# A recurrent image layer and a state-space layer on one core: the second layer's order of issue from another table of priorities

## The chip, the cores and the metric

The kernel runs on one core of a Trainium2 chip. The metric is the device time of one execution in microseconds; the median of several runs counts. The engines are TensorE (PE, with its weight loads PEld), VectorE (DVE), ScalarE (ACT), GpSimd (POOL) and SyncE (SP), which here does nothing but issue DMAs. "us" is a microsecond.

## The reference

The input is 16 images of 64 x 64 pixels with 128 channels, in float32. Two layers follow one another, each with a group norm before and a residual sum after:

```python
x = x + L0(group_norm(x))      # a 2-D recurrent layer: 5 gates, swept along the diagonals
x = x + L1(group_norm(x))      # a state-space layer (Mamba) on the 4096 pixels in order,
                               # once forward and once backward, the two results summed
```

The change touches only the second layer. For each image and direction it computes, with 256 inner channels and 16 states:

```python
xz = x @ in_w.T;  xc, z = split(xz)
xc = silu(conv1d(xc, 4 taps))
dt, Bm, Cm = split(xc @ x_w.T);  dt = softplus(dt @ dt_w.T + dt_b)
for t in pixels:                                 # per channel d and state s
    h[d, s] = exp(-dt[t, d] * exp(A_log[d, s])) * h[d, s] + dt[t, d] * Bm[t, s] * xc[t, d]
    y[t, d] = sum_s h[d, s] * Cm[t, s]
out = ((y + xc * D) * silu(z)) @ out_w.T
```

## The kernel before

The first layer takes the first 1.6 ms and is not touched. The second layer works in passes. A pass is 512 pixels of one image in one direction, so an image has 16 passes: 0 to 7 forward, 8 to 15 backward (`second` in the code). A forward pass ends by storing its `y` (`spill`); the backward pass of the same pixels fetches it (`recall`), adds it (`again`), multiplies by the gate (`finish`), turns it (`back`) and projects it (`project`). So a backward pass has more matmuls than a forward one. During an image's forward passes the next image is read: `read_load`, `read_turn` (TensorE), `read_take` (ACT), `read_stats` (DVE), in eight chunks; then `normal` makes the norm's factors and `normalise` (ACT, L1068) applies them, chunk by chunk.

A pass has 2 halves of 128 channels (h) and 16 states (s), that is 32 scans on DVE (`scan`, L1305), each over 128 partitions x 512 pixels. Each scan needs a decay factor, which ACT makes as an exponential (`decay`, L1251, tile `da`). There are two kinds of states:

- States 0 to 3 (letter X in the plan): POOL makes the product that drives the scan (`drive`, L1259) in a tile `group`, of which there are two buffers. TensorE turns the scanned group (`turned`, L1337, tile `ptg`), ACT copies it (`turned_take`, L1345), and TensorE weighs it by Cm and sums it (`weigh`, L1352).
- States 4 to 15 (letter R): TensorE makes the drive of four states at a time (`drive_rows`, L1285, tile `hps`); DVE scans into `hst`; POOL multiplies two states by their Cm rows (`out_of`, L1328, tile `hc`); TensorE sums by transposes into `py` (`sums`, L1365).

Further operations of a pass: `conv` (TensorE, L1122, tile `pp`, two passes ahead), `silu` and `softplus` (ACT, in "sessions", since each needs its function table loaded), `xproj`, `dtproj`, `bturn`, `times` (POOL, L1232, tile `dtx`), `turn`, `skip`, `gate`. The carried states go from pass to pass by small DMAs (`keep`, `keep_group`); rows of Bm and Cm are spread over the partitions by DMAs (`spread`).

Nothing of this runs in the order of the source. When the kernel is built, `order_of_issue` makes a list of all operations of all 256 passes with what each needs, and `simulate` plays them through with a cost table and picks, whenever an engine is free, the ready operation with the smallest key whose buffers are free. The key of an operation of pass i (the image's first pass counts 16 times the images before it) is

```python
at = NS * i
urgency = at + URGENCY[name][second][args if who is None else ()]
```

So a pass is worth 16 units, a small number goes first, and an engine never idles while something for it is ready. `read_*` of chunk n have the `at` of pass n of the image before, and `normalise` of chunk k has that of pass 8 + k. The list that comes out is issued as it stands: it fixes the order in each engine's queue and in SP's queue of DMAs, and each queue is worked in that order. Buffers go round by operation order too (`RINGS`: 2 `group`, 3 `hst`, 3 `hc`, 9 `da`, 1 `quad`, 1 `xl`; three shared banks for `misc`). The order of states within a pass is a constant of its own, `ORDER`.

Of the kernel before, what the change touches and what calls it, by code (L numbers as in the profile page):

```python
# [44 lines left out]
def units_of(order):  # L45

    count = {}
    for x in order:
# [4 lines left out]
        else:  # L53
# [37 lines left out]
        {(0, 0): -19.08, (0, 1): 208.77, (0, 2): 213.67, (0, 3): 242.61, (1, 0): -194.98, (1, 1): -170.3,  # L91
         (1, 2): -208.38, (1, 3): -208.83},
        {(0, 0): 148.19, (0, 1): 250, (0, 2): 249.74, (0, 3): 231.08, (1, 0): -185.59, (1, 1): -186.03,
         (1, 2): -176.29, (1, 3): -177.49},
    ),
    "xproj": (
        {(): -6.34},
        {(): 83.3},
    ),
    "xproj_take": (  # L100
        {(): 46.52},
        {(): -25.9},
    ),
    "rows": (
        {(): 10.88},
        {(): -173.37},
    ),
    "bturn": (
        {(): 216.27},
        {(): -247.72},  # L110
    ),
    "bturn_take": (
        {(): -10.16},
        {(): 155.72},
    ),
    "dtproj": (
        {(0,): -166.35, (1,): -49.09},
        {(0,): -234.94, (1,): -199.34},
    ),
    "times": (  # L120
        {(0,): -141.19, (1,): -141.5},
        {(0,): -190.57, (1,): -223.42},
    ),
    "turn": (
        {(0,): 231.47, (1,): -199.74},
        {(0,): 155.15, (1,): 101.59},
    ),
    "turn_take": (
        {(0,): 35.4, (1,): 33.43},
        {(0,): 227.22, (1,): 227.05},  # L130
    ),
    "skip": (
        {(0,): -85.09, (1,): 194.24},
        {(0,): -59.43, (1,): 211.98},
    ),
    "spread": (
        {("b", 0): 55.31, ("d", 0): 221.01, ("c", 0): 249.78, ("c", 1): 249.59, ("d", 1): -104.59, ("c",
         2): 74.43, ("c", 3): 179.65, ("b", 1): 235.3, ("d", 2): 178.23, ("c", 4): 117.53, ("c", 5):
         216.75, ("k", 0): 205.82},
        {("b", 0): 49.04, ("d", 0): 82.05, ("c", 0): 58.5, ("c", 1): 225.69, ("d", 1): 85.64, ("c", 2):  # L140
         -52.53, ("c", 3): -84.56, ("b", 1): -71, ("d", 2): 188.69, ("c", 4): -46.09, ("c", 5): 139.95,
         ("k", 0): 79.7},
    ),
    "drive": (
        {(0, 0): -117.16, (1, 0): -45.65, (0, 1): -106.02, (1, 1): 204.54},
        {(0, 0): -55.01, (1, 0): -101.65, (0, 1): 78.56, (1, 1): 78.33},
    ),
    "decay": (
        {(0, 0): 214.71, (4, 0): 231.6, (5, 0): 235.97, (6, 0): 250, (7, 0): 244.04, (1, 0): -226.9, (8,
         0): 242.45, (9, 0): 229.56, (10, 0): 250, (11, 0): 196.68, (2, 0): 245.22, (12, 0): 142.99, (13,  # L150
         0): 196.62, (14, 0): 218.85, (15, 0): 250, (3, 0): 235.27, (4, 1): 237.55, (5, 1): 56.83, (6,
         1): 236.39, (7, 1): 200.04, (0, 1): 59.98, (8, 1): 241.45, (9, 1): 238.35, (10, 1): 238.37, (11,
         1): 237.94, (1, 1): 48.96, (12, 1): 223.29, (13, 1): 109.79, (14, 1): 109.58, (15, 1): 193.48,
         (2, 1): 244.06, (3, 1): 190.67},
        {(0, 0): 219.27, (4, 0): 159.93, (5, 0): 228.42, (6, 0): 227.96, (7, 0): 233.04, (1, 0): 162.12,
         (8, 0): 236.54, (9, 0): 145.98, (10, 0): -139.12, (11, 0): -88.73, (2, 0): -99.75, (12, 0):
         157.46, (13, 0): 250, (14, 0): 156.85, (15, 0): 167.22, (3, 0): 239.69, (4, 1): 187.28, (5, 1):
         236.16, (6, 1): 225.96, (7, 1): 248.99, (0, 1): 67.98, (8, 1): 248.77, (9, 1): 49.99, (10, 1):
         242.8, (11, 1): 168.72, (1, 1): 67.45, (12, 1): 163.7, (13, 1): 244.57, (14, 1): 244.31, (15,
         1): 176.22, (2, 1): 178.59, (3, 1): 181.09},  # L160
    ),
    "scan": (
        {(0, 0): -215.99, (4, 0): -197.78, (5, 0): -201.82, (6, 0): 171.7, (7, 0): -200.28, (1, 0):
         208.99, (8, 0): 81.27, (9, 0): 69.78, (10, 0): 50.84, (11, 0): 80.97, (2, 0): -179.33, (12, 0):
         -157.48, (13, 0): -159.07, (14, 0): -158.42, (15, 0): -158.71, (3, 0): -148.7, (4, 1): 17.61,
         (5, 1): 34.08, (6, 1): 7.6, (7, 1): 7.23, (0, 1): 145.62, (8, 1): 26.88, (9, 1): 56.47, (10, 1):
         26.63, (11, 1): 52.08, (1, 1): 203.51, (12, 1): 173.49, (13, 1): 174.73, (14, 1): 173.35, (15,
         1): 173.11, (2, 1): 173.02, (3, 1): -185.61},
        {(0, 0): 211.65, (4, 0): 208.82, (5, 0): 213.32, (6, 0): 210.34, (7, 0): 234.88, (1, 0): 234.81,
         (8, 0): 82.08, (9, 0): 81.92, (10, 0): 11.04, (11, 0): 61.9, (2, 0): 80.26, (12, 0): 96.06, (13,  # L170
         0): 93.07, (14, 0): 44.04, (15, 0): 82.19, (3, 0): 68.39, (4, 1): -115.05, (5, 1): -159.13, (6,
         1): -144.43, (7, 1): -169.42, (0, 1): -152.48, (8, 1): -158.76, (9, 1): -192.29, (10, 1):
         -192.53, (11, 1): -193.7, (1, 1): 178.94, (12, 1): 148.84, (13, 1): 136.94, (14, 1): 136.65,
         (15, 1): 184.35, (2, 1): 182.44, (3, 1): 227.69},
    ),
    "scatter": (
        {("d", 0): -98.3, ("d", 1): 226.02, ("d", 2): -35.02, ("k", 0): 142.02},
        {("d", 0): 197.57, ("d", 1): 181.75, ("d", 2): -137.41, ("k", 0): 53.02},
    ),
    "drive_rows": (  # L180
        {(0, 0): 86.02, (1, 0): -84.84, (2, 0): 123.21, (0, 1): 206.34, (1, 1): 117.75, (2, 1): 194.74},
        {(0, 0): 241.28, (1, 0): -59.19, (2, 0): -162.71, (0, 1): -157.55, (1, 1): -215.22, (2, 1):
         175.52},
    ),
    "keep": (
        {(0, 0): 250, (1, 0): -11.9, (2, 0): 227.54, (3, 0): -221.6, (4, 0): 195.72, (5, 0): -92.62, (0,
         1): 62.29, (1, 1): 169.33, (2, 1): 81.35, (3, 1): -229.04, (4, 1): 142.26, (5, 1): -18.73},
        {(0, 0): -186.63, (1, 0): 100.75, (2, 0): 123.12, (3, 0): -226.46, (4, 0): 126.26, (5, 0):
         182.78, (0, 1): -126.19, (1, 1): 179.51, (2, 1): -247.02, (3, 1): -146.55, (4, 1): -45.3, (5,
         1): 57.7},  # L190
    ),
    "out_of": (
        {(0, 0): 6.28, (1, 0): 110.81, (2, 0): 0.41, (3, 0): 46.99, (4, 0): 204.64, (5, 0): 230.6, (0,
         1): 26.46, (1, 1): 164.53, (2, 1): -138.94, (3, 1): -244.66, (4, 1): -239.51, (5, 1): -149.12},
        {(0, 0): -174.66, (1, 0): -174.81, (2, 0): 72.48, (3, 0): 7.85, (4, 0): 129.81, (5, 0): 102.68,
         (0, 1): -122.95, (1, 1): -122.04, (2, 1): -117.06, (3, 1): -192.11, (4, 1): -39.91, (5, 1): 57.1},
    ),
    "sums": (
        {(0, 0): 147.01, (1, 0): 204.95, (2, 0): 18.42, (3, 0): 110.12, (4, 0): -165.71, (5, 0): -154.21,
         (0, 1): 227.07, (1, 1): 180.09, (2, 1): 194.99, (3, 1): 242.48, (4, 1): 216.64, (5, 1): -169.16},  # L200
        {(0, 0): -212.32, (1, 0): -162.81, (2, 0): -161.63, (3, 0): -161.82, (4, 0): -157.85, (5, 0):
         -158.54, (0, 1): 73.85, (1, 1): 109.31, (2, 1): 81.83, (3, 1): 248.19, (4, 1): 249.43, (5, 1):
         249.81},
    ),
    "keep_group": (
        {(0, 0): -194.35, (0, 1): -163.44},
        {(0, 0): -239.33, (0, 1): -182.43},
    ),
    "turned": (
        {(0, 0, 0): -203.27, (0, 0, 1): 190.03, (0, 0, 2): 9.82, (0, 0, 3): -96.4, (0, 1, 0): 229.53, (0,  # L210
         1, 1): -154.5, (0, 1, 2): -157.58, (0, 1, 3): -113.93},
        {(0, 0, 0): -157.81, (0, 0, 1): 123.6, (0, 0, 2): -144.76, (0, 0, 3): -39.63, (0, 1, 0): 248.86,
         (0, 1, 1): 248.61, (0, 1, 2): 248.52, (0, 1, 3): 239.67},
    ),
    "turned_take": (
        {(0, 0, 0): 113.8, (0, 0, 1): 75.95, (0, 0, 2): 42.34, (0, 0, 3): 42.24, (0, 1, 0): 247.32, (0,
         1, 1): 153.61, (0, 1, 2): 153.43, (0, 1, 3): 222},
        {(0, 0, 0): 64.54, (0, 0, 1): 69.77, (0, 0, 2): 68.43, (0, 0, 3): 67.62, (0, 1, 0): -249.7, (0,
         1, 1): -214.46, (0, 1, 2): 155.94, (0, 1, 3): 155.85},
    ),  # L220
    "weigh": (
        {(0, 0): -250, (0, 1): -131.3},
        {(0, 0): -179.49, (0, 1): -150.84},
    ),
    "finish": (
        {(0,): 43.55, (1,): 250},
        {(0,): -158.64, (1,): 234.04},
    ),
    "spill": (
        {(): 111.19},  # L230
        {},
    ),
    "read_load": (
        {(): -159.46},
        {},
    ),
    "read_turn": (
        {(): 120.8},
        {},
    ),  # L240
    "read_take": (
        {(): 144.64},
        {},
    ),
    "read_stats": (
        {(): 1.05},
        {},
    ),
    "gate": (
        {},  # L250
        {(0,): -158.22, (1,): -164.04},
    ),
    "recall": (
        {},
        {(): -141.83},
    ),
    "again": (
# [1238 lines left out]
```

## Time and profile before

| | us |
|---|---|
| median of 3 runs | 12678.93 (12673.02 to 12680.4) |
| the profiled execution, its own time | 12716.73 |
| its span, first to last instruction | 12714.9 |
| first `times` of the second layer | 1580.8 after the start |
| pass 9 to 14 of any image from 1 to 14, each | 43.98 |

The TensorE clock granted is 0.993 of full speed over the span. In the second layer the profile's engine totals per 1000 us are about 960 us for PE, 905 for DVE, 835 for ACT and 932 for POOL. The profile's tables by stretch have a line for each stretch of time: its bounds and length, then busy time and number of instructions of PE, PEld, DVE, ACT and POOL, then the granted PE clock, the share of DMA engines and GB/s. A line of a timeline has the start, the time from the start of the first to the end of the last of a run of like instructions, engine, source line, tiles and count, and in brackets the idle time before it and what ended it. PE's instructions overlap: a matmul that is shown with 275 ns can start 109 ns after the one before it.

### The profile page before, as it was taken

Reading aid. Unit: us, or ns where it says so; the run is one execution under the profiler, and the core shown is the slowest. Engines: PE = TensorE matmul, PEld = TensorE weight load, DVE = VectorE, ACT = ScalarE, POOL = GpSimd, SP = SyncE. Lnnn points to the kernel's source line nnn. Section 1 sums busy time; section 2 is a strip of 40 time slices with the busy share of each in tenths; the row PEclk is TensorE's granted clock in tenths of the full one; section 3 lists DMA queues with packets and bytes.
Section 4 is the critical chain, followed back from the end, with each engine's and each line's share of the span. In section 5 each row is a group of like instructions: output and inputs, shape, how many; then the busy total and the mean of one; then the engine's idle time right before and its main releaser. Section 6 shows DMA issues by size and latency. Waiting matters only on the chain. (4 is left out here: it accounts for less than half of the span.)

```text
span 12714.9 us, 322475 instructions
## 1 busy us (share of the span) xinstructions
PE 12144.3 (96%) x128820; PEld 9452.5 (74%) x128820; DVE 11120.1 (87%) x11409; ACT 9944.8 (78%) x15935; POOL 10600.8 (83%) x4868
## 2 busy tenths in 40 slices
PE   8999999999999999999999999999999999999999
PEld 7666777777777777777777777777777777777777
DVE  6676599998989899999999998999989898989998
ACT  3444488888888888888888888888888888888887
POOL 0111199999999999999999998999999999999998
PEclk8999999999999999999999999999999999999999
DMA  4222155555555555555555555555555565556564
GB/s 151 54 57 55 49 157 162 159 159 158 164 160 156 160 161 158 159 165 156 164 159 160 158 164 158 163 161 156 160 159 160 156 163 156 158 158 164 155 163 138
DMA packets 2320784, 1885.93 MB, mean 148 GB/s; under 512 B 1537697, under 2 KB 1883313, under 8 KB 2319281
## 3 DMA queue, kind: packets, MB, share of 16 engines
q1 hardware_dynamic: 2241328, 1830.04, 52.2%
q10 hardware_dynamic: 77952, 35.24, 1.2%
q8 instruction: 1017, 16.66, 0.5%
q14 instruction: 487, 3.98, 0.1%
HBM read 1698.25 MB, written 164.30 MB: 146 GB/s over the span
## 5 line engine op out<-in xcount | busy, mean ns | idle before, releaser
L1328 POOL TENSOR_TENSOR hc<-hst,cr 128x1024 f32<-128x1024 f32 x3072 | 7380.5, 2430 | 416.6 <-DVE hst L1305 308.6
L1305 DVE TENSOR_TENSOR_SCAN hst<-da,carry,hps 128x512 f32<-128x512 f32 x5376 | 6452.1, 1261 | 497.7 <-issue 266.5
L1251 ACT ACTIVATE da<-dt,A_log_sb 128x512 f32<-128x512 f32 x8192 | 5386.9, 710 | 907.0 <-DVE hst L1305 814.8
L1365 PEld LDWEIGHTS py<-ident,hc 128*128 128x128 f32 x24576 | 2760.8, 141 | 685.1 <-issue 322.3
L1365 PE MATMUL py<-ident,hc 128*128 128x128 f32 x24576 | 3136.2, 275 | 139.2 <-POOL hc L1328 135.8
L1259 POOL TENSOR_TENSOR group<-dtx,br 128x1024 f32<-128x1024 f32 x1024 | 2448.6, 2405 | 150.2 <-PE ptg L1337 80.0
L1305 DVE TENSOR_TENSOR_SCAN group<-da,carry,group 128x512 f32<-128x512 f32 x1792 | 2236.1, 1267 | 203.7 <-ACT da L1251 199.5
L1285 PEld LDWEIGHTS hps<-d,dtxt 32*128 32x128 f32 x49152 | 1522.7, 186 | 731.7 <-issue 389.2
L1285 PE MATMUL hps<-d,dtxt 32*128 32x128 f32 x49152 | 1804.9, 283 | 211.1 <-DVE hst L1305 128.3
L1122 PE MATMUL pp<-xT,wk 128*128 128x512 f32 x4096 | 1994.7, 600 | 2.4 <-ACT dt L1226 1.2
L1345 ACT COPY ht<-ptg 128x512 f32<-128x512 f32 x2048 | 1130.4, 588 | 414.8 <-PE ptg L1337 390.3
L889 POOL TENSOR_TENSOR a_f<-a_f,c 128x288 f32<-128x288 f32 (+40 forms) x254 | 211.3, 832 | 1338.2 <-ACT a_f L881 1272.4
L1337 PE MATMUL ptg<-ident,group 128*128 128x128 f32 x8192 | 1154.3, 276 | 50.2 <-DVE group L1305 27.0
L1337 PEld LDWEIGHTS ptg<-ident,group 128*128 128x128 f32 x8192 | 926.5, 141 | 273.5 <-issue 106.2
L1122 PEld LDWEIGHTS pp<-xT,wk 128*128 128x128 f32 x4096 | 681.6, 191 | 420.6 <-issue 390.4
L1305 DVE TENSOR_TENSOR_SCAN hst<-da,hps 128x512 f32<-128x512 f32 x768 | 876.3, 1200 | 124.4 <-POOL hc L1328 38.2
L1232 POOL TENSOR_TENSOR dtx<-dt,xc 128x512 f32<-128x512 f32 x512 | 650.4, 1286 | 198.1 <-ACT dt L1226 168.2
L1251 ACT ACT_TABLE_LOAD x527 | 676.1, 1283 | 9.7
L1365 PE MATMUL py<-ddiag,xc 128*128 128x128 f32 x4096 | 579.3, 284 | 12.3 <-ACT y L1412 11.3
L1352 PE MATMUL py<-ht,k 128*32 128x128 f32 x16384 | 557.7, 276 | 0.8
L1365 PEld LDWEIGHTS py<-ddiag,xc 128*128 128x128 f32 x4096 | 496.8, 191 | 54.4 <-ACT y L1412 15.6
L1216 PE MATMUL pv<-dbl,dt_wT 128*128 128x256 f32 x2048 | 531.2, 392 | 0.2 <-DVE st L1056 0.2
(112 smaller groups left out, 12155.8 us busy)
## 6 DMA issues: line engine op xcount, KB each, us to landing
cr<-rows SPq DMA_DIRECT2D x1536, 512.0 KB
d<-d SPq DMA_DIRECT2D x768, 448.0 KB
br<-rows SPq DMA_DIRECT2D x512, 512.0 KB
k<-k SPq DMA_DIRECT2D x256, 256.0 KB
yf<-y SPq DMA_DIRECT2D x128, 512.0 KB
yl<-yf SPq DMA_DIRECT2D x128, 512.0 KB
carry<-hst SPq DMA_DIRECT2D x3072, 1.0 KB
xs<-in_x_dram SPq DMA_DIRECT2D x64, 512.0 KB
```

What stands on the lines that cost most here:

```text
L1122: nc.tensor.matmul(self.ps["conv", h], lhsT=wk[:, k, h * P : (h + 1) * P], rhs=xT[self.b % 2][:, t0 : t0 + T], start=(k == 0), stop=(k == ...
L1216: nc.tensor.matmul(pv[:, q * TQ : (q + 1) * TQ], lhsT=dt_wT[:, q, h * P : (h + 1) * P], rhs=self.dbl, start=True, stop=True,)
L1232: nc.gpsimd.tensor_mul(self.dtx[h], self.dt[h], self.xc[h])
L1251: nc.scalar.activation(t, self.dt[h], AF.Exp, scale=amat[:, h, s : s + 1])
L1259: nc.gpsimd.tensor_mul(both[:, m : m + 2, :], bc(self.dtx[h], 1, 2), self.brow[q])
L1285: nc.tensor.matmul(part[:, j, :, :], lhsT=self.dtxt[h][rows, j, :], rhs=dg[rows, j + r, :, :], start=True, stop=True, skip_group_check=True,)
L1305: nc.vector.tensor_tensor_scan(t[:, self.rev], self.da.pop((s, h))[:, self.rev], dbx[:, self.rev], 0.0 if self.first else carry[:, self.d, ...
L1328: nc.gpsimd.tensor_mul(self.hc[g, h], self.hst[g, h].rearrange("p t m -> p m t"), self.crow[g])
L1337: nc.tensor.transpose(pt[:, k, :], self.group[g, h][:, t0 : t0 + TB, :].rearrange("p t s -> p (t s)"), ident,)
L1345: nc.scalar.copy(t, self.ps.pop(("turned", g, h, j)))
L1352: nc.tensor.matmul(self.py[h][q * TB : (q + 1) * TB, j * P : (j + 1) * P], lhsT=cd[:, GX * j + q, :], rhs=self.ht[g, h, j][:, q, :], start ...
L1365: nc.tensor.matmul(self.py[h][:, cols], **{"start": False, "stop": False, **how}, skip_group_check=True)
```

## The change

The table `URGENCY` gets other numbers, nearly all of them. Names, arguments and meaning of the entries, the operations, the cost table, buffers and `ORDER` stay as they are; so do the instructions of every engine, but for their order. Of the diff, the entries that the text below speaks of (in each entry the first table is for forward passes, the second for backward ones):

```diff
     "drive": (
-        {(0, 0): -117.16, (1, 0): -45.65, (0, 1): -106.02, (1, 1): 204.54},
-        {(0, 0): -55.01, (1, 0): -101.65, (0, 1): 78.56, (1, 1): 78.33},
+        {(0, 0): -56.91, (1, 0): -57.77, (0, 1): 215.02, (1, 1): 247.85},
+        {(0, 0): 171.33, (1, 0): 123.34, (0, 1): 160.79, (1, 1): 118.53},
     ),
     "decay": (
-        {(0, 0): 214.71, (4, 0): 231.6, (5, 0): 235.97, (6, 0): 250, (7, 0): 244.04, (1, 0): -226.9, (8,
...
+        {(0, 0): 224.88, (4, 0): 226.48, (5, 0): 240.06, (6, 0): 188.37, (7, 0): 250, (1, 0): 113.5, (8,
...
     "scan": (
-        {(0, 0): -215.99, (4, 0): -197.78, (5, 0): -201.82, (6, 0): 171.7, (7, 0): -200.28, (1, 0):
-         208.99, (8, 0): 81.27, (9, 0): 69.78, (10, 0): 50.84, (11, 0): 80.97, (2, 0): -179.33, (12, 0):
-         -157.48, (13, 0): -159.07, (14, 0): -158.42, (15, 0): -158.71, (3, 0): -148.7, (4, 1): 17.61,
-         (5, 1): 34.08, (6, 1): 7.6, (7, 1): 7.23, (0, 1): 145.62, (8, 1): 26.88, (9, 1): 56.47, (10, 1):
-         26.63, (11, 1): 52.08, (1, 1): 203.51, (12, 1): 173.49, (13, 1): 174.73, (14, 1): 173.35, (15,
-         1): 173.11, (2, 1): 173.02, (3, 1): -185.61},
...
+        {(0, 0): -110.99, (4, 0): -110.09, (5, 0): -105.1, (6, 0): -105.34, (7, 0): -105.61, (1, 0):
+         181.32, (8, 0): 19.6, (9, 0): 19.21, (10, 0): -80.71, (11, 0): 7.49, (2, 0): 40.13, (12, 0):
+         -108.17, (13, 0): -102.34, (14, 0): -10.85, (15, 0): -108.25, (3, 0): -48.47, (4, 1): -48.83,
+         (5, 1): -68.91, (6, 1): -83.82, (7, 1): -96.92, (0, 1): -31.74, (8, 1): -33.58, (9, 1): -38.05,
+         (10, 1): -40.96, (11, 1): -50.07, (1, 1): 200.94, (12, 1): -50.19, (13, 1): -87.76, (14, 1):
+         -88.26, (15, 1): -91.09, (2, 1): -5.51, (3, 1): -86.39},
...
     "read_load": (
-        {(): -159.46},
+        {(): 20.22},
...
     "read_turn": (
-        {(): 120.8},
+        {(): 64.91},
...
     "read_take": (
-        {(): 144.64},
+        {(): 21.14},
...
     "read_stats": (
-        {(): 1.05},
+        {(): -142.37},
...
     "normal": (
...
-        {(): 74.69},
+        {(): 29.66},
...
     "normalise": (
...
-        {(): 57.35},
+        {(): 32.48},
...
     "session": (
-        {(0,): 241.85, (1,): 239.93},
-        {(0,): 173.19, (1,): 69.9},
+        {(0,): 219.11, (1,): 226.41},
+        {(0,): 244.88, (1,): 9.25},
```

## The prediction

> **What bounds the kernel now.** I read the page first (engine totals), then busy time by stretch, one stretch per pass of the second layer, cut where POOL starts the pass's first `dtx` product (L1232); then the timeline of all engines in the worst pass, and TensorE's timeline in a backward pass. The page says only that four engines are nearly full:
>
> ```profile
> span 12714.9 us, 322475 instructions
> PE 12144.3 (96%) x128820; PEld 9452.5 (74%) x128820; DVE 11120.1 (87%) x11409; ACT 9944.8 (78%) x15935; POOL 10600.8 (83%) x4868
> ```
>
> The stretches say which of them bounds which pass. They are passes 1, 2, 6, 7, 8 and 10 of image 8; columns: length, busy PE, PEld, DVE, ACT, POOL.
>
> ```profile
> 7163.04:7209.38 46.34, 41.61 (x484) 32.86 (x480) 40.54 (x39) 37.52 (x61) 40.77 (x20) 1.00 0.68 185
> 7209.38:7256.80 47.42, 41.16 (x475) 31.68 (x474) 41.28 (x40) 44.32 (x69) 40.43 (x19) 1.00 0.50 144
> 7380.15:7420.60 40.45, 38.55 (x456) 30.17 (x456) 37.62 (x33) 34.28 (x55) 40.45 (x20) 1.00 0.59 159
> 7420.60:7462.46 41.86, 38.38 (x456) 30.11 (x456) 38.98 (x34) 35.48 (x55) 40.49 (x19) 1.00 0.57 160
> 7462.46:7509.24 46.78, 43.29 (x518) 33.66 (x518) 40.25 (x36) 35.49 (x57) 45.27 (x21) 1.00 0.58 161
> 7553.22:7597.20 43.98, 43.97 (x496) 34.76 (x492) 40.16 (x36) 36.35 (x56) 40.64 (x18) 1.00 0.56 161
> ```
>
> See three regimes. A forward pass in its stride (the third and fourth lines) is POOL's: POOL works 40.45 to 40.49 us of it and the pass lasts 40.45 to 41.86. A backward pass (the last) is TensorE's: 43.97 us busy of 43.98, and six passes of every image have that length to 0.06 us. Passes 1, 2 and 8, where the direction turns, belong to nobody: no engine fills them. The last image has no successor to read, and its passes 1 and 2 are shorter:
>
> ```profile
> 12039.14:12082.49 43.35, 38.81 (x462) 30.42 (x458) 39.30 (x35) 36.36 (x57) 40.42 (x20) 1.00 0.58 158
> 12082.49:12122.92 40.43, 38.73 (x456) 30.23 (x456) 37.38 (x33) 33.85 (x54) 40.43 (x19) 1.00 0.60 162
> ```
>
> So reading and normalising the next image is what stretches passes 1 and 2. How it does so, in pass 2 of image 8:
>
> ```profile
> 7226.80 3.62 ACT L1068 ACTIVATE xT<-xT,shift_l,scale_l 128x512 f32<-128x512 f32 x5
> ...
> 7231.03 2.51 DVE L1305 TENSOR_TENSOR_SCAN group<-da,carry,group 128x512 f32<-128x512 f32 x2 [0.52 <-ACT da L1251]
> ...
> 7233.60 0.66 PE L1337 MATMUL ptg<-ident,group 128*128 128x128 f32 x4 [0.79 <-DVE group L1305]
> ...
> 7237.86 2.38 POOL L1259 TENSOR_TENSOR group<-dtx,br 128x1024 f32<-128x1024 f32 x1 [4.74 <-PE ptg L1337]
> ```
>
> Five normalisations in a row hold ACT; the scans of `group` wait for their decay, TensorE's turns wait for the scans, and POOL's next `drive` waits 4.74 us for one of two `group` buffers.
>
> **The change, part by part.** No instruction is added or removed; every engine's queue is put in another order, DMA issue on SP included. So the cost of an edit is not a duration but what becomes late, and I cost it by regime, per image, from the means of images 1 to 14 in the same stretches: pass 0 38.45; passes 1 and 2 94.66; passes 3 to 7 206.62; pass 8 47.80; passes 9 to 14 263.90; pass 15 44.12; in all 695.55 us.
>
> *Backward passes 9 to 15.* TensorE cannot be better fed: the gain is nothing unless its own work shrinks. It can change a little, since a switch between kinds of matmul has a price:
>
> ```profile
> 7564.11 1.02 PE L1122 MATMUL pp<-xT,wk 128*128 128x512 f32 x2
> 7565.07 1.17 PE L1285 MATMUL hps<-d,dtxt 32*128 32x128 f32 x32
> ...
> 7567.10 1.02 PE L1122 MATMUL pp<-xT,wk 128*128 128x512 f32 x2
> 7567.96 0.60 PE L1337 MATMUL ptg<-ident,group 128*128 128x128 f32 x4
> ```
>
> A pair of `pp` takes 0.96 us of the queue ahead of the 32-row `hps`, 0.86 us ahead of `ptg`, which keeps the shape: 0.10 us for a switch. A backward pass has 17 switches (counted in its list). I can't see how many the new order has; two more or fewer a pass are 0.2 x 7 x 16 = 22 us, of either sign; I take 0. The Trainium skill speaks against treating an order of matmuls as free: "TensorEngine Tiling (Array Packing)", Key Properties, says that a change of tiling mode drains the engine. The row agrees and gives the price; the page has none. On headroom the skill and the row differ: "Perfetto Trace Analysis", Identifying the Most-Contended Engine, would judge TensorE by its weight loads and not by matmul busy time. By that, 34.76 of 43.98 us, an estimate of 9.2 us a pass could still be had by a better order, 9.2 x 7 x 16 = 1030 us in all. I don't count it: the batches of this timeline follow one another at the same distance wherever they stand (0.87 to 0.96 us for eight `py` of 128 columns, the longer ones beside a switch, and once 1.04), which is how a full queue looks.
>
> *Forward passes 3 to 7.* 206.62 less five times POOL's 40.5 us is 4.1 us an image that a perfect order would give. A loss is as possible: TensorE works 38.4 to 38.9 us of these passes, so it has only some 1.9 us to give before POOL starves. I take 0.
>
> *Pass 8.* 47.80 us with POOL busy for 45.27: at most 2.5 us. I take 0.
>
> *Passes 1 and 2.* 94.66 against 83.78 in the last image: 10.9 us an image are the price of the next image's reading, of which the work itself would fit beside POOL (POOL's own 81 us are a floor 13.7 us below). The table moves this part most visibly. `normal` (DVE) goes from 74.69 to 29.66 while most forward scans move to between -111 and 40, so at pass 2 its key, 128 + 29.66 = 158, stands behind nearly all scans (32 + 40 = 72 or less), where it stood at 203 ahead of those at 32 + 209 = 241 and 32 + 204 = 236. That is for a gain: scans are no longer held up by it. Against it: `normalise` goes from 57.35 to 32.48, so for chunk k its key at pass 2 is 160 + 16k, and with decays of that pass at 32 + 225 = 257 seven chunks come ahead of decay (0, 0), where four did (185 + 16k against 247): the same burst on ACT, 7 x 0.70 = 4.9 us by the 3.62 us row. The ends are 0 and 10.9 us; neither row is nearer, since the last image leaves the whole of the work out and not only its bunching, and I take half, 5.4 us, in 15 images: 82 us.
>
> *Start and end.* The first image's passes 0 and 1 take 79 us together, near two of POOL's; the last pass and the tail take 85 us after POOL's last `dtx`. I take 0 for both; a few us are possible.
>
> The sum: the profiled execution's own time is 12716.73 us, of which the span is 12714.9. 12716.7 - 82 = 12635. The median of the runs is 12678.93, 0.997 of it, so 12635 x 0.997 = 12597 us.
>
> **The rivals.** *More than half.* If the new order spreads the burst and also straightens the forward passes, the ceiling is 13.7 + 4.1 + 2.5 = 20.3 us an image, 305 us in 15 images; 10.9 + 3.3 (half of the other two) give 213 us, or 12467 us. For it: POOL, TensorE and DVE each have the room in passes 1 and 2. Against it: one `xl` buffer and two `group` buffers stay, and the keys of `normalise` keep the burst.
>
> *Slower: TensorE's queue starves POOL in the forward passes.* The queue is in order; a `py` or `ptg` batch that waits for POOL or DVE holds back the `hps` behind it, then the scans, then POOL. The planner that made the order bills TensorE too little: its cost table adds up to 42.64 us for a backward pass, where the row shows 43.98, and to 36.7 for a forward one, where the rows show 38.4 to 38.9. It therefore sees 4.0 us of room in a forward pass (40.7 of its own POOL costs) where there are 1.9, and a longer search uses up room that it believes in. The point from which this decides is a hold-up of over 1.9 us a pass. Its price by the nearest rows, the 1.35 us that POOL waits for `hst` twice in pass 1: one such wait in each of passes 3 to 7 is 1.35 x 5 x 16 = 108 us, 12679 + 108 = 12787 us. For it: three engines are over 90% busy there. Against it: the present order, made with the same costs, stays within 1 us of POOL's floor.
>
> *Nothing.* The keys move but work goes wherever an engine is idle, so the bunching and the floors stay: 12679 us, give or take 25.
>
> *A stall in backward passes.* DVE, POOL and ACT have 3.3 us or more to spare there, so one extra wait is absorbed; 0.5 us a pass would be 56 us, 12735.
>
> **How the numbers follow.** What a measurement of this kernel can tell from no change is about 0.2%, 25 us. The forecast, a gain from 25 to some 165 us (12515 to 12654 is its own range), has 0.44; the larger gain 0.13; nothing 0.14; the slower forward passes 0.22; the backward stall 0.07. Faster is 0.57, the same 0.14, slower 0.29. The range runs from the larger gain's 12467 to just over the forward rival's 12787: 12465 to 12800, and I leave some 0.06 below and 0.1 above.
>
> **What would show it.** In the profile after: passes 1 and 2 together at about 89 us instead of 94.66, with POOL's longest wait on `ptg` under 4.74; passes 9 to 15 still 43.9 to 44.2 us with TensorE busy throughout; passes 3 to 7 still within 40.5 to 42.5. Wrong would be: backward passes under 43.5 (the work of TensorE is not fixed) or over 44.5 (it is no longer fed); forward passes over 42.5 (the slower rival); or equal busy and idle times everywhere.

## The result, and the profile after

The changed kernel takes 12606.47 us in the median of 4 runs (12602.26 to 12615.94), the kernel before 12676.69 us in the runs beside them (12673.02 to 12680.4). The ratio is 0.9945, with a 95% interval from 0.9932 to 0.9959: 70 us or 0.55% faster. The forecast was 12597 us, with all of its gain in passes 1 and 2. The size came out right, by luck: in two profiles taken for comparison (below), passes 1 and 2 give 22 of 62 us, and most of the gain lies elsewhere.

The page of the changed kernel hides the change as well as that of before did. Its span and engine totals:

```profile
span 12600.5 us, 322464 instructions
PE 12132.4 (96%) x128820; PEld 9488.3 (75%) x128820; DVE 11138.1 (88%) x11409; ACT 9942.7 (79%) x15935; POOL 10601.1 (84%) x4868
```

The busy time by stretch, for the same six passes of image 8 as in the prediction (1, 2, 6, 7, 8 and 10; columns: length, busy PE, PEld, DVE, ACT, POOL, PE clock, DMA share, GB/s):

```profile
7114.09:7159.33 45.24, 41.19 (x480) 32.33 (x477) 40.77 (x39) 38.14 (x61) 40.54 (x20) 1.00 0.66 184
7159.33:7206.28 46.95, 42.59 (x478) 33.93 (x476) 41.01 (x40) 43.58 (x69) 40.47 (x20) 0.96 0.57 151
7330.66:7371.48 40.82, 38.52 (x456) 30.13 (x456) 38.62 (x33) 35.04 (x55) 40.48 (x19) 1.00 0.60 159
7371.48:7412.53 41.05, 38.84 (x456) 30.15 (x456) 38.29 (x33) 35.19 (x55) 40.53 (x20) 1.00 0.57 162
7412.53:7457.73 45.20, 43.36 (x506) 33.83 (x506) 40.41 (x36) 35.78 (x57) 45.20 (x21) 1.00 0.57 167
7501.50:7545.19 43.69, 43.66 (x496) 34.88 (x492) 40.22 (x36) 36.34 (x57) 40.66 (x18) 1.00 0.58 161
```

Passes 1 and 2 lost about a microsecond and a half together, where 5.4 were forecast. Pass 8 went from 46.78 to 45.20 us, which is POOL's own busy time, so in this image no wait of POOL is left there. The backward pass is still TensorE's alone (43.66 of 43.69), but it is 0.29 us shorter with the same 496 matmuls. The PE clock in pass 2 is 0.96, where the lines of before have 1.00; an experiment below follows this up.

The timeline of pass 2 shows the picture of before again, a little worse at its end:

```profile
7176.19 3.62 ACT L1066 ACTIVATE xT<-xT,shift_l,scale_l 128x512 f32<-128x512 f32 x5
...
7180.42 1.28 DVE L1303 TENSOR_TENSOR_SCAN group<-da,carry,group 128x512 f32<-128x512 f32 x1 [1.75 <-ACT da L1249]
...
7187.35 2.39 POOL L1257 TENSOR_TENSOR group<-dtx,br 128x1024 f32<-128x1024 f32 x1 [5.24 <-PE ptg L1335]
```

The burst of `normalise` on ACT, the scan that waits for its decay, and POOL's wait for a `group` buffer are all there. POOL's wait is 5.24 us, where 4.74 stood before and less was forecast.

### The profile page after: what moved, and what is told of

The parts are those of the page before. It is cut to its first block, busy times and chain, and to the rows that moved or that the text cites. A ratio compares the mean times of both kernels' runs of the same rounds, so it can differ in the third digit from the quotient of the medians.

```text
span 12600.5 us, 322464 instructions
## 1 busy us (share of the span) xinstructions
PE 12132.4 (96%) x128820; PEld 9488.3 (75%) x128820; DVE 11138.1 (88%) x11409; ACT 9942.7 (79%) x15935; POOL 10601.1 (84%) x4868
## 5 line engine op out<-in xcount | busy, mean ns | idle before, releaser
L1120 PE MATMUL pp<-xT,wk 128*128 128x512 f32 x4096 | 1954.9, 599 | 1.7 <-ACT dt L1224 1.2
```

The source lines that it names most:

```text
L1120: nc.tensor.matmul(self.ps["conv", h], lhsT=wk[:, k, h * P : (h + 1) * P], rhs=xT[self.b % 2][:, t0 : t0 + T], start=(k == 0), stop=(k == ...
```

## Where the time went

The first profiled execution of before lay 40 us above its median, so I measured both kernels again and compare these two executions. In the experiments the kernel before runs at 12736 us, 0.5% above the first comparison; ratios are therefore compared, not times. The unchanged copies:

> The kernel before, unchanged, profiled a second time. Its first profiled execution took 12716.7 us, 40 us over the median of its other runs, so the profiles of before and after stand 114 us apart where the medians stand 70. If the 40 us are chance of that one execution, the second one takes 12665 to 12690 us and it is seen where they lay (forward passes 3 to 7 below 206.6 us an image, or the tail below 85 us). If the profile itself costs them, it takes 12710 to 12720 again. In both cases the backward passes 9 to 14 stay at 43.98 us.

Measured: 0.9995 of the kernel before [0.9985, 1.0005], span 12726.0 us. The profiled execution took 12727.8 us, above both values named, but not longer than the other executions of the same copy (median 12730). So the profile itself costs nothing here; what the first one's 40 us were stays open. The backward passes stayed at 43.98 us.

> After, unchanged, for a second profile and a second measure of its gain. The forward passes 3 to 7 took 204.7 us an image in its first profile; with one batch moved in backward passes alone (the second dtproj behind drive_rows), on another chip, they took 207.4, as before's did there (207.5). If the order itself shortens these passes, they are at least 1.5 us shorter than before's again wherever both are profiled; if that difference was chance of the execution, they lie anywhere from 204.5 to 207.5, while passes 9 to 13 (43.70), pass 8 (45.5 to 46.1 against 47.6 to 47.8) and the 72 us after POOL's last dtx come back. Ratio to before 0.993 to 0.996.

Measured: 0.9945 [0.9931, 0.9959] over five runs, span 12664.2 us, 61.8 us less. I cut both traces at POOL's first `dtx` of every pass and take means over images 1 to 14:

| stretch | before again, us | changed again, us | per image | all 16 images | forecast |
|---|---|---|---|---|---|
| passes 1 and 2 | 94.61 | 93.28 | -1.33 | -22 | -82 |
| of these, pass 1 | 47.09 | 46.06 | -1.03 | -17 | |
| of these, pass 2 | 47.51 | 47.23 | -0.28 | -5 | |
| passes 3 to 7 | 207.45 | 207.05 | -0.40 | -9 | 0 |
| pass 8 | 47.57 | 46.25 | -1.32 | -24 | 0 |
| passes 9 to 15 | 308.04 | 307.78 | -0.26 | -4 | 0 |
| up to the second layer's first `dtx` | 1581.9 | 1579.5 | | -2 | 0 |

The column for all images adds the first and the last image, which I measured by themselves. The rows for passes 3 to 7 can't be trusted to the microsecond: five executions of before's order gave 206.6 to 207.5 us there and six of the changed order 204.7 to 207.6. Passes 1 and 2 are firm: 94.61 to 94.81 against 93.18 to 93.28 us. So is pass 8 in its sign: 47.5 to 47.8 against 45.5 to 46.5 us. (Copies that an experiment below edits in another place are counted with their order.)

The gain of passes 1 and 2 lies in pass 1. In the first two profiles too, pass 1 went from 47.22 to 45.62 us and pass 2 from 47.44 to 47.61. What shrank in pass 1 is a wait of TensorE, which reads the next image's chunks there through the one `xl` buffer and stands until each chunk has landed: 2.30 us an image in before's second profile, 1.50 in the changed kernel's (2.46 and 1.17 in the first two). The sixth chunk of image 8, before and after:

```profile
7193.97 0.63 PE L1046 MATMUL pt<-ident,xl 128*128 128x128 f32 x4 [0.88 <-DMA xl<-x]
```

```profile
7144.26 0.60 PE L1044 MATMUL pt<-ident,xl 128*128 128x128 f32 x4
```

In each of the 14 profiles of this study pass 1 is longer in those images where this wait is longer, by 0.8 to 1.5 us for each microsecond. No experiment changes this wait alone, so that it is the cause fits the traces and isn't shown.

## The experiments

An execution's whole list of operations is made before anything is issued. Most edits below only move entries of that list, by a small generator `rearranged` around `order_of_issue(B)`; the diffs, shortened, show what it moves. Three questions were open: what holds passes 1 and 2, why a backward pass is shorter, and what happened in pass 8.

**Is it the burst of `normalise`?** The changed kernel, with the eight steps moved to passes 3 to 10, one each:

```diff
+        if name == "normalise":
+            held[who, args[0]] = op
+            continue
+        if name == "turned_take" and args == (0, 1, 0):
+            b, i = divmod(who, NP)
+            if (b + 1, i - 2) in held:
+                yield held.pop((b + 1, i - 2))
```

> After, with the eight normalisations of the next image moved in ACT's queue from one burst in pass 2 to one chunk in each of passes 3 to 10, in front of the ACT copies of turned state group (0, 1). Theory A, that of the prediction (the burst holds back the decays, then the group scans, the turns and POOL, which waits 5.2 us on ptg in pass 2): pass 2 falls from 47.6 us to about 44 and the wait on ptg to under 2 us, the other passes stay; 15 images x 3.6 = 54 us, so about 12550 us. Theory B (not the burst but the norm's short chain before it and the reading itself stretch passes 1 and 2): pass 2 changes by less than 1 us, passes 3 to 10 lose up to 0.7 us each, so 12600 to 12690 us.

Measured: 0.9933 [0.9916, 0.9949]; passes 1 and 2 together 91.67 us instead of 93.28 (pass 2 45.94 instead of 47.23), passes 3 to 7 206.86, pass 8 46.06. In pass 2 VectorE's wait for the decay fell from 2.58 to 0.53 us, as the chain in the prediction has it, but POOL's wait on `ptg` only from 5.14 to 4.21. The burst is worth 1.3 us an image in pass 2, 1.6 with pass 1, not half of 11. By its median this is the fastest kernel of the study; its interval overlaps that of the changed kernel, so that it beats it isn't shown.

**Is it the root with its table loads, or the statistics?** In the first of the two kernels the norm's square is made by VectorE and the square root is left out from image 1 on; in the second, seven of the eight statistics of an image are left out.

```diff
-        nc.scalar.activation(std, pv, AF.Sqrt, bias=eps)
-        nc.vector.reciprocal(scale, std)
+        nc.vector.reciprocal(scale, pv)          # from image 1 on
```

> After, with the square root and the square of the next images' norm taken off ACT: the square is made on DVE, and the root is left out (the reciprocal of the variance stands for it), so two ACT table loads of 1.28 us and DVE's wait of 1.84 us for the root go from pass 2 of 15 images. Theory A (the norm's chain through ACT is what delays the group scans of pass 2): pass 2 falls by 2 to 3 us from 47.6 and the time by 30 to 45 us. Theory B (passes 1 and 2 are long because the reading of a whole image adds work to DVE, ACT and TensorE in them): pass 2 falls by less than 1 us.

Measured: 0.9934 [0.9916, 0.9952]; passes 1 and 2 93.31 us. VectorE's wait for the root (1.84 us) went, but TensorE now waited 1.20 us for VectorE's square, where it had waited 0.48 for ScalarE's. What pass 2 won, 0.7 us, pass 1 lost, where TensorE's wait for the chunks grew from 1.50 to 2.09.

```diff
-            nc.vector.bn_stats(norm[b][:, c, :], raw[b, c])
+            if b == 0 or c == 0:
+                nc.vector.bn_stats(norm[b][:, c, :], raw[b, c])
```

> After, with the statistics of only the first of the eight chunks of each next image (the other seven bn_stats on DVE are left out and the norm is made from one chunk), so 7 x 0.67 = 4.7 us of DVE work leave passes 1 and 2. Theory A (with the reading, DVE has more work in passes 1 and 2 than POOL: 2 x 38.3 + 8 x 0.67 + the norm's 3.4 = 85.4 us against POOL's 81): passes 1 and 2 fall from 93.2 by 3 to 5 us. Theory B (DVE's load is not it, POOL waits for turns behind ACT and TensorE work): they fall by less than 1 us.

Measured: 0.9951 [0.9933, 0.9969]; passes 1 and 2 92.68 us. Seven statistics of 0.69 us of VectorE's time bring 0.6 us, and POOL's wait on `ptg` grows to 6.17. No single load holds these passes.

**Is it the half clock?** In the changed kernel's trace TensorE's granted clock falls to half for 3413 ns (sometimes twice that) in pass 2 of 13 of 15 images, 54.6 us in all; in the repeated execution 44.4 us, in before's none. (Pass 1 has half clock in every profile, 6.8 us in before's second one and 20.5 in the changed kernel's.) The stretches begin mostly within 1.6 us of the norm's last small matmul. A window of 6 us there (its clock is 0.72), and a batch of TensorE's timeline in it, which takes 2.8 us at full clock in other runs:

```profile
7172.00:7178.00 6.00, 6.00 (x51) 5.28 (x44) 5.53 (x7) 5.96 (x10) 4.76 (x3) 0.72 0.88 223
```

```profile
7172.53 4.46 PE L1363 MATMUL py<-ident,hc 128*128 128x128 f32 x24
```

So I kept TensorE at work around the norm with eight matmuls whose result nobody uses:

```diff
+        if later:
+            idle_work(4)     # 4 x matmul(pm[:, P:2*P], lhsT=gavg, rhs=ident)
         nc.tensor.matmul(mean, lhsT=gavg, rhs=mv[:, :, 0], start=True, stop=True)
+        if later:
+            idle_work(4)
```

> The changed kernel, with four extra full-array matmuls (128x128) on each side of the norm's first tiny matmul, from image 1 on; their result is not used. In the changed kernel's trace TensorE's granted clock falls to half for 3.41 us in the third pass (pass 2) of 13 of 15 images, mostly within 1.6 us of the norm's last tiny matmul, 44.4 us of half clock in all; the norm stands there between batches on small tiles, with waits of 0.46 and 0.48 us. Theory C (the norm's thin work draws the half clock, and this costs pass 2 about half of 3.41 us): with TensorE kept at work through the norm the half-clock stretches of pass 2 fall from 44.4 us to under 15, pass 2 from 47.2 to 45.5-46.2 us less up to 0.9 us that the extra matmuls cost, and the time by 10 to 30 us: ratio to before 0.992-0.994. Rival D (the clock is drawn by the small-tile batches around the norm, not by the norm): the stretches stay at 35-55 us, ratio 0.9945-0.9955. Rival E (the clock is not on the path, POOL and VectorE are): stretches gone, pass 2 unchanged within 0.3 us.

Measured: 0.9971 [0.9960, 0.9982], slower than the changed kernel. The half clock near the norm is gone (pass 2: 13.7 us in all instead of 44.4, all of it 12 us or more behind the norm; pass 1 has 27.3 us), and passes 1 and 2 take 95.13 us instead of 93.28, pass 2 alone 48.50 instead of 47.23. In image 8 pass 2 has its full clock, the same busy time of TensorE as with the half clock (42.59 above), and is longer:

```profile
7207.57:7255.73 48.16, 42.65 (x494) 34.04 (x492) 41.08 (x40) 43.73 (x70) 40.51 (x20) 1.00 0.58 146
```

VectorE's timeline shows what got longer. It waits inside the norm for TensorE's mean, behind the added matmuls (columns: start, length, then the instruction, and in brackets the idle time before it):

```profile
7219.86 0.16 DVE L742 TENSOR_TENSOR dev_l<-mv,pm_l 128x1 f32<-128x1 f32 x1 [1.64 <-PE pm_l L734]
7221.86 0.16 DVE L750 RECIPROCAL scale_l<-std_l 128x1 f32<-128x1 f32 x1 [1.84 <-ACT std_l L748]
```

In the changed kernel the first of these waits is 0.47 us:

```profile
7170.44 0.15 DVE L732 TENSOR_TENSOR dev_l<-mv,pm_l 128x1 f32<-128x1 f32 x1 [0.47 <-PE pm_l L730]
7172.44 0.16 DVE L740 RECIPROCAL scale_l<-std_l 128x1 f32<-128x1 f32 x1 [1.84 <-ACT std_l L738]
```

The theory of the half clock predicted a gain, and none came: full clock came back near the norm and no time with it. That the half clock costs nothing isn't shown, since this run adds work and delays the norm too.

The next two ran with it. One moves the norm, besides the late `normalise`, out of the small matmuls to between two convolution batches; the other does the reverse to the kernel before, where the norm stands between convolutions.

```diff
+        if name == "normal" and who > 1:
+            norm[who] = op
+            continue
...
+        if name == "conv" and args == (0, 1) and i == 4 and b + 1 in norm:
+            yield norm.pop(b + 1)
```

> The changed kernel, with the eight normalise steps of an image moved to passes 3 to 10, one each, and with the norm itself moved out of the run of small-tile batches to between the second and the third convolution batch of the same pass, from image 2 on. Theory C and the burst together: half-clock stretches of pass 2 fall from 41.0 us (the run with the late normalise alone) to under 10, pass 2 from 45.9 to 44.5-45.3 us, ratio to before 0.991-0.9925, and below the changed kernel's 0.9945. If the clock isn't on the path: 0.9933 again, as with the late normalise alone.

Measured: 0.9944 [0.9932, 0.9957]; half clock in pass 2 halved (20.5 us), passes 1 and 2 at 94.24 us, 2.57 more than with the late `normalise` alone, 1.50 of them in pass 2, where the norm stands. The expected gain did not come. VectorE's wait for the mean grew from 0.47 to 2.97 us in the mean over the images, since the mean's matmul now stands behind four convolution matmuls in TensorE's queue:

```profile
7213.11 0.16 DVE L752 TENSOR_TENSOR dev_l<-mv,pm_l 128x1 f32<-128x1 f32 x1 [2.98 <-PE pm_l L750]
```

```diff
+        op = order.pop(at)                      # at: place of normal of image b
+        to = order.index(("turn_take", (b - 1) * NP + 2, (1,), []))
+        order.insert(to + 1, op)
```

> The kernel before, with the norm alone moved ahead from between two convolution batches to directly behind the skip's small-tile batch, as in the changed kernel's order, from image 2 on. Theory C: half-clock stretches appear in pass 2 (none before; 30 to 50 us in all), pass 2 grows from 47.5 to 48.3-49.2 us, the time by 10 to 25 us: ratio 1.001-1.002. If the place of the norm has nothing to do with the clock: no stretches in pass 2, ratio 0.9995-1.0005.

Measured: 0.9995 [0.9987, 1.0004]; no half clock in pass 2, passes 1 and 2 94.93 us. So the norm's place behind small matmuls does not draw the half clock by itself; here a convolution follows 1.2 us after the norm begins, in the changed order 6.8 us after. My expectation missed.

The pair of waits in the norm is what these runs have in common. VectorE works its queue in order, and pass 2 follows the time that it stands there, though not one for one: +2.50 us of waiting and +1.50 us of pass 2 with the norm between convolutions, +1.17 and +1.27 with the added matmuls (their own work included), -1.07 and -0.69 without the root. Before's order, at the same place, shows the wait that the change shortened by 0.74 us, for 0.28 us of pass 2:

```profile
7222.27 0.16 DVE L734 TENSOR_TENSOR dev_l<-mv,pm_l 128x1 f32<-128x1 f32 x1 [1.21 <-PE pm_l L732]
```

**Can the preparation be hidden elsewhere?** In every trace so far passes 1 and 2 are 9.3 to 12.7 us longer than in the last image, which prepares no successor. The last experiment moves most of the preparation: five of eight reads to passes 3 to 7, the norm to pass 8, `normalise` to passes 8 to 15.

```diff
+        for c in range(3, NCH):
+            place = order[at["turn", w + c, (1,)]][3]
+            move(("read_turn", b + 1, (c,)), ("sums", w + c - 1, (2, 1)), place)
...
+            move(("read_take", b + 1, (c,)), ("decay", w + c, (7, 0)))
+            move(("read_stats", b + 1, (c,)), ("scan", w + c - 1, (13, 1)))
+        move(("normal", b + 1, ()), ("drive_rows", w + NCH - 1, (2, 1)), ...)
+        for c in range(NCH):
+            move(("normalise", b + 1, (c,)), ("turned_take", w + NCH - 1 + c, (0, 1, 0)))
```

> The changed kernel, with the preparation of the next image taken out of passes 1 and 2 as far as its single buffer allows: of the eight reads (four transposes, a copy, a statistic each) three stay in pass 1 and five move to passes 3 to 7, one each; the norm moves to pass 8, the eight normalise steps to passes 8 to 15, one each; the residual load of pass 8 moves behind the last read. Same operations and buffers otherwise. In every trace so far passes 1 and 2 take 9.3 to 12.7 us longer in images that prepare a next one than in the last image, which prepares none (changed kernel: 93.28 against 82.09 us). Theory P (the place makes the price: in passes 3 to 7 POOL is busy 40.5 of 41 us, TensorE and VectorE have about 2.5 and 3 us free): passes 1 and 2 fall from 93.3 to 84-88 us, passes 3 to 7 rise by at most 0.7 us each from 207.1 to at most 210.5, passes 8 to 15 by at most 0.3 each; ratio to before 0.987-0.992. Rival Q (a read stops the in-order queues wherever it stands, 1.2 us or more each): passes 1 and 2 fall the same, passes 3 to 7 rise to 213 or more, ratio 0.993-0.998.

Measured: 0.9948 [0.9934, 0.9961], no gain over the changed kernel; theory P's 0.987 to 0.992 missed. Passes 1, 2, 5 and 8 of image 8:

```profile
7136.15:7179.16 43.01, 39.58 (x467) 30.68 (x462) 38.62 (x35) 36.07 (x56) 40.53 (x19) 1.00 0.59 169
7179.16:7222.66 43.50, 39.61 (x467) 30.98 (x465) 39.48 (x35) 35.07 (x58) 40.46 (x20) 1.00 0.62 156
...
7307.04:7349.41 42.37, 38.75 (x460) 30.55 (x460) 39.10 (x35) 35.42 (x57) 40.44 (x19) 1.00 0.58 154
...
7432.47:7480.59 48.12, 44.10 (x512) 34.55 (x512) 41.03 (x40) 38.62 (x61) 45.32 (x22) 1.00 0.57 155
```

Per image, passes 1 and 2 fall by 5.48 us (93.28 to 87.80), as theory P has it; passes 3 to 7 rise by 3.27 (207.05 to 210.32), 0.65 for each read, within its bound; but pass 8 rises by 2.52 (46.25 to 48.77), and there P missed. The norm, now in pass 8, took its waits along, from a place where nobody was full to one where POOL is:

```profile
7442.33 0.15 DVE L763 TENSOR_TENSOR dev_l<-mv,pm_l 128x1 f32<-128x1 f32 x1 [0.49 <-PE pm_l L761]
7444.33 0.16 DVE L771 RECIPROCAL scale_l<-std_l 128x1 f32<-128x1 f32 x1 [1.84 <-ACT std_l L769]
```

0.49 + 1.84 us of waiting stand beside a price of 2.52. That they are the price isn't shown: a `normalise` step moved into this pass too, and the last image, which has no norm in it, took 48.43 us for its pass 8 in this run as well, with TensorE waiting 1.8 us for the recalled `y`. The half clock of pass 2 is down to 3.4 us here, and the time is that of the changed kernel with 44.4; again no gain came with the clock.

**Why is a backward pass shorter?** Both orders keep TensorE full there, with 17 changes of tile form in each of the passes 9 to 13. What differs is which batches are neighbours. Part of TensorE's timeline in the changed kernel, where both halves of `pv` follow the full-array `py`:

```profile
7585.11 1.89 PE L1214 MATMUL pv<-dbl,dt_wT 128*128 128x256 f32 x8
7586.93 1.17 PE L1283 MATMUL hps<-d,dtxt 32*128 32x128 f32 x32
7588.03 1.08 PE L1157 MATMUL pd<-xc,x_wT_sb 128*64 128x256 f32 x8
```

In before's the first half of `pv` stands between `pd` and `hps`, the second behind `pbt`. I put the second half behind `hps` in the changed kernel, which makes 19 changes of form out of 17:

```diff
+        if name == "dtproj" and args == (1,) and NCH < who % NP < NP - 1:
+            held = op
+            continue
+        yield op
+        if held and name == "drive_rows":
+            yield held
+            held = None
```

> After, with one TensorE batch moved in the stretches of passes 9 to 13: the second dtproj (full array) goes behind the 32-row drive_rows that follows it, so that it stands between two small-tile batches. Same instructions. Theory A (on TensorE's full queue an excursion to a small tile shape costs 0.09 us going in and 0.06 to 0.10 us coming out, and that, not waiting, is why these passes last 43.70 us after and 43.98 before): each of these passes grows by 0.20 us to 43.9 with TensorE still busy throughout, in all 0.2 x 5 or 6 x 16 = 16 to 19 us. Theory B (the difference of 0.28 us between before and after comes of short waits): the length changes by less than 0.05 us, and the time by nothing that can be measured.

Measured: 0.9971 [0.9959, 0.9983], and the usual backward pass 44.00 us instead of 43.69. The same instructions in TensorE's timeline:

```profile
7590.44 1.13 PE L1228 MATMUL pv<-dbl,dt_wT 128*128 128x256 f32 x4
7591.50 1.08 PE L1171 MATMUL pd<-xc,x_wT_sb 128*64 128x256 f32 x8
```

Moving one batch of four matmuls costs 0.31 us a pass where 0.20 was expected, and 25 us in all by the medians (12694.68 against 12669.33). The reverse in the kernel before, `dtproj` (0) ahead of `xproj` in passes 9 to 13 (the names of the list; the batches are `pv` and `pd`):

```diff
+                if name == "dtproj" and args == (0,) and (who - 1) % NP > NCH:
+                    held.insert(0, held.pop())
```

> Before, with two neighbours in TensorE's queue exchanged in passes 9 to 13 of every image: dtproj(0) goes ahead of xproj, so that xproj (128x64), drive_rows (32x128) and bturn (64x64) stand side by side instead of with a full-array batch between the first two. Theory A (what the backward passes gain is fewer excursions between full-array and small-tile batches, 0.2 to 0.3 us for each): 43.98 becomes 43.70 to 43.80 and the time falls by 15 to 22 us, this one part of the change done alone. Theory B (dtproj must wait for its bank when it comes 1 us earlier): TensorE shows a wait at pv and the passes stay at 43.9 to 44.2.

Measured: 0.9995 [0.9986, 1.0004]. The usual backward pass goes to 43.87 us, a third of the way to 43.69, pass 9 rises to 44.29 and pass 14 falls to 43.55; passes 9 to 14 together are 0.5 us an image shorter, about 8 us in all, which the time doesn't show beyond its noise. That neighbours matter is shown; which of them make the whole 0.29 us isn't. In pass 14 the changed order has 19 changes of form to before's 17, and there it is longer, 44.22 us against 43.98.

**Pass 8.** In before TensorE waits there for the recalled `y`, with `hps` and then POOL behind it:

```profile
7497.07 1.12 PE L1365 MATMUL py<-yl,ident 128*128 128x512 f32 x2 [1.45 <-DMA yl<-yf]
```

I moved that batch six operations of TensorE back in the kernel before:

```diff
+        if name == "again" and args == (0,) and who % NP == NCH:
+            held = op
+            continue
+        if held and name == "gate":
+            yield held
+            held = None
```

> Before, with one TensorE operation moved in pass 8 of every image: again(0), the sum of the first fetched forward result, goes six operations later, to just before the gate matmuls. Theory A (pass 8 is long because TensorE's queue stands 1.45 us at again until the fetch of yl lands, with drive_rows and then scans and POOL behind it): pass 8 falls from 47.8 to about 46.4 us, TensorE's wait on yl is gone, and the time falls by 1.4 x 16 = 22 us to about 12655. Theory B (pass 8 is POOL's, which has 45.3 us of work in it, and DVE waits for hst buffers from POOL): pass 8 changes by less than 0.3 us and the time by less than 5 us.

Measured: 0.9992 [0.9983, 1.0001]. The wait is gone and pass 8 falls only from 47.57 to 47.12 us, a third of what the changed order brings. POOL's timeline shows why. The pass ends where POOL starts the next pass's `dtx`, and for that it waits for `dt`, the softplus on ACT. In the kernel before, and with the moved batch:

```profile
7509.24 1.28 POOL L1232 TENSOR_TENSOR dtx<-dt,xc 128x512 f32<-128x512 f32 x1 [0.79 <-ACT dt L1226]
```

```profile
7502.46 1.28 POOL L1247 TENSOR_TENSOR dtx<-dt,xc 128x512 f32<-128x512 f32 x1 [1.64 <-ACT dt L1241]
```

In the mean over images 1 to 14 the moved batch took POOL's wait for `hst` in pass 8 from 1.20 to 0.02 us, and the wait for `dt` behind it grew from 0.79 to 1.63. The changed order shortens both, to 0.63 and 0.20 us, and its wait for `ptg` from 0.19 to 0.04, together 1.3 us, as much as the pass. TensorE's wait for `y` is not shorter there (1.03 us, 0.93 before), so that wait isn't what the change won. The second session of a backward pass, the softplus, did get a smaller key (69.9 to 9.25), which fits an earlier `dt`; no run tests it alone.

## Why the prediction was right, and where it was not

- **The sum.** 82 us were forecast, 70 measured. That is luck: terms taken as zero made up for the one that was too large. In the repeated pair passes 1 and 2 give 22 us, pass 8 24, passes 3 to 7 9, passes 9 to 15 4 and the start 2.
- **Passes 1 and 2, the only term.** 5.4 us an image were forecast, 1.3 to 1.4 came. The step that failed is "scans are no longer held up by it": I ranked `normal`'s key against the scans' keys, as though a lower rank made it late. A key only chooses among what is ready. In the changed trace the norm still stands between scans on VectorE and stops them for 0.47 + 1.84 us, where before stopped them for 1.21 + 1.84. Pass 2, where it stands, won 0.28 us in the repeated pair and nothing in the first. The rest came in pass 1 (1.03 us), with TensorE's wait for the chunks of the next image 0.80 us shorter. The keys of `read_load` and `read_turn`, which moved as well, have no term in the sum.
- **Half of the preparation's price as the gain.** That price did not fall at all: passes 1 and 2 of the last image, which prepares nothing, went from 83.70 to 82.09 us in the two repeated executions, so the preparation cost 10.9 us before and 11.2 after. Over five executions of before's order the last image gave 83.0 to 84.3 us, over nine of the changed one (all its experiments leave the last image alone there) 81.6 to 83.7. So some gain in passes 1 and 2 is there without preparation too, as far as one image per trace can tell: there POOL waited 2.28 us in pass 1 for a carried state that a DMA brings, and after the change it doesn't. Its rows in the changed kernel's trace:

```profile
11934.60:11975.46 40.86, 38.74 (x463) 30.30 (x458) 38.29 (x34) 35.16 (x56) 40.51 (x19) 1.00 0.57 167
11975.46:12016.16 40.70, 38.52 (x456) 30.13 (x456) 38.34 (x33) 34.97 (x55) 40.51 (x20) 1.00 0.60 161
```

- **The burst stays.** Right, and so is its chain, but it is worth 1.3 to 1.6 us, not most of the price. The sign named for it was wrong: POOL's wait on `ptg` grew to 5.24 us.
- **Pass 8.** The ceiling of 2.5 us was right and the value 0 was not: 1.3 us an image, 24 us in all, the largest term beside passes 1 and 2. The waits that were left for the change to shorten are POOL's, for `hst` and `dt`. Half of the ceiling, as taken for passes 1 and 2, would have given 20.
- **Backward passes.** The sign named, 43.9 to 44.2 us with TensorE busy throughout, failed narrowly at 43.69, but not as far as the 43.5 that would have meant wrong. The bound of 22 us either way holds (4 us in the repeated pair, 18 in the first). The price of 0.10 us for a switch was low: two more cost 0.31 us in the experiment. Counting them was not enough either: at 17 in both orders the passes differ by 0.29 us. The Trainium skill's rule ("TensorEngine Tiling (Array Packing)", Key Properties: a change of tiling mode drains the engine) was the right warning, and the moved batch, with two more changes, came to 0.31 us a pass.
- **Forward passes 3 to 7, the start and the end.** Right at nothing: -0.4 us an image in passes 3 to 7, within their scatter, -2 us at the start and -0.2 from the last image's pass 14 to the end. The rival in which TensorE's queue starves POOL did not come; POOL's rows are where they were.
- **The headroom by weight loads.** "Perfetto Trace Analysis" of the Trainium skill, Identifying the Most-Contended Engine, which names weight loads beside MFU (the share of peak arithmetic) as measures of TensorE's headroom, would by the weight loads have promised the estimated 1030 us in the backward passes; leaving it out was right, they gave 4 to 18 us.

## What to carry to other kernels

A priority says who goes first among the ready, so the place of an operation must be read from the order that results, and an in-order engine that waits inside a short dependent chain (two waits of 0.5 and 1.8 us here) holds up what stands behind it: pass 2 followed each microsecond of change in these waits with 0.4 to 1.1 us. When a wait is taken away, look for the next one behind it: POOL's wait for `hst` in pass 8 fell by 1.2 us and the one for `dt` grew by 0.8. When several stretches have a ceiling each, share the expected gain out among them; taking one at half and the others at zero gave the right sum for the wrong reasons. And split a stretch before explaining it: passes 1 and 2 as one row hid that the gain lay in pass 1 and the explanation in pass 2.

## What the runs showed of the hardware that I had not expected

- **Half clock without a window of idling.** In the changed kernel the granted clock fell to half in pass 2 for 3413 or 6827 ns at a time, though the idle gaps of TensorE in the 3.4 us ahead of each drop added up to 0.9 to 2.0 us. The Trainium skill, "TensorE: Matmul & The Clock Gate", Part 1: The HAM clock gate, gives a window of 3413 ns, which agrees to the nanosecond, and ties the drop to an idle window, which these traces don't show. What goes with most of the drops here is a run of small-tile and one-column matmuls without a convolution. Matmuls added around the norm took the drops there away; moving the norm alone in before's order didn't bring them. What draws them stays open.
- **A table load on each side of the root.** In the changed kernel's ACT timeline two loads of 1.28 us enclose the root, and the first is most of VectorE's 1.84 us. Without the root the kernel wasn't measurably faster.

```profile
7170.85 1.28 ACT L738 ACT_TABLE_LOAD   x1
7172.15 0.26 ACT L738 ACTIVATE std_l<-pm_l,eps 128x1 f32<-128x1 f32 x1
7172.43 1.28 ACT L1249 ACT_TABLE_LOAD   x1
```
